# Transposing x and the adjacency on VectorE in 32x32 blocks instead of on TensorE

## The chip, the cores and the metric

One core of one Trainium2 chip. The metric is device time in microseconds (us) of one launch; lower is better. "Same" means within 2% of the other kernel.

## The reference, cut to what matters

128 graphs of 128 nodes and 768 features, one attention layer with 12 heads of 64 behind a layer norm and a relu, with the adjacency as bias and mask:

```python
h = jnp.maximum(_layernorm(x, axis=-1), 0.0)            # x: (128, 128, 768) float32
q, k, v = split(h @ Wq + bq), split(h @ Wk + bk), split(h @ Wv + bv)
scores = einsum('bhqd,bhkd->bhqk', q, k) / sqrt(64)
scores = where(adj > 0, scores + beta * adj, -9e15)      # adj: (128, 128, 128)
x = x + einsum('bhqk,bhkd->bhqd', softmax(scores), v)
```

## The kernel before

It works on groups of four graphs. The three projections run as "slices" (first half of q and k, then v, then second half of q and k); a slice is 15 block products of a fast matrix multiplication, each eight TensorE instructions into a PSUM bank. Each bank is emptied ("evicted") by VectorE or ScalarE before it is written again. The attention of the group and the preparation of the next group (layer norm, transposition of h, bias) are woven in between products. The parts:

```python
def norm(G, g):                                   # layer norm of one graph, rows on partitions
    for s in range(2):
        nc.vector.bn_stats(st[:, s, :], t[:, s * VH:(s + 1) * VH])
    nc.vector.bn_aggr(mv, st)
    nc.vector.tensor_scalar(ve, mv[:, 1:2], EPS, None, op0=ALU.add)
    nc.gpsimd.tensor_tensor(rstd, ve, nhalf, ALU.pow)            # 128x1
    nc.vector.tensor_scalar(t, t, mv[:, 0:1], rstd, op0=ALU.subtract, op1=ALU.mult)

def to_hT(G, r, k):                               # six a group
    for c in range(2):
        for g in range(2):
            nc.tensor.transpose(p[:, c, g, :], xg[G, 2 * r + g][:, at:at + P], ident)
    nc.scalar.activation(t, p..., AF.Relu)

# ... make_bias: cap and square the adjacency, then
    for g in range(GRP):
        nc.tensor.transpose(p[:, g, :], nb[:, g, :], ident)
    nc.scalar.activation(biasT[G], p, AF.Copy, scale=ISCALE)

def product(G, sl, n):                            # cut: eight matmuls into bank p, then for v
    # first use of an output block: out = bias +- p ; later uses: out = out +- p
    nc.vector.tensor_tensor(o, o, got, ALU.add if sign > 0 else ALU.subtract)
```

The code counts products from 0. The banks of a V slice are used in the order c, a, b, c, d, a, c, b, d, c, a, b, c, a, b. That is the order in which their evictions stand in VectorE's queue.

Of the kernel before, what the change touches and what calls it, by code (L numbers as in the profile page):

```python
# [9 lines left out]
F32 = mybir.dt.float32  # L10
I32 = mybir.dt.int32
U8 = mybir.dt.uint8
AF = mybir.ActivationFunctionType
# [82 lines left out]

@with_exitstack
def direct(ctx, tc, x, adj, wq, bq, wk, bk, wv, bv, beta, out, bad):

# [13 lines left out]
    ISCALE = math.sqrt(HD)  # L113
    assert N == P and 2 * HD == P and B % GRP == 0 and W == 512 and NC == 6 and GRP == 4
# [8 lines left out]
    def load_x(G, g):  # L123
        xg[G, g] = work.tile([P, D], F32, tag="x", name=f"x_{G}_{g}")
        nc.sync.dma_start(xg[G, g], x[G * GRP + g])
# [4 lines left out]
    make_identity(nc, ident)  # L130
    nhalf = const.tile([P, 1], F32, name="nhalf")
# [16 lines left out]
    def load_block(sl, k, j, t):  # L148
        rows = slice(k * 2 * P, (k + 1) * 2 * P)
        if sl == "v":  # L150
            nc.scalar.dma_start(t, wv[rows, j * 2 * P:(j + 1) * 2 * P].rearrange("(c p) n -> p c n", p=P))
        else:
            oc = j + 3 * int(sl[2])
            for i, w in enumerate((wq, wk)):
                nc.scalar.dma_start(t[:, :, i * P:(i + 1) * P],
                                    w[rows, oc * P:(oc + 1) * P].rearrange("(c p) n -> p c n", p=P))
# [23 lines left out]
    nc.scalar.dma_start(beta_c, beta[None, :].to_broadcast([P, 1]))  # L180
    bqk = const.tile([P, 2, NC], F32, name="bqk")
# [5 lines left out]

    def norm(G, g):
        t = xg[G, g]
        st = stat.tile([P, 2, nc.vector.BN_STATS_DIM], F32, tag="st", name=f"st_{G}_{g}")  # L190
        for s in range(2):
            nc.vector.bn_stats(st[:, s, :], t[:, s * VH:(s + 1) * VH])
        mv = stat.tile([P, nc.vector.BN_AGGR_DIM], F32, tag="mv", name=f"mv_{G}_{g}")
        nc.vector.bn_aggr(mv, st)
        ve = stat.tile([P, 1], F32, tag="ve", name=f"ve_{G}_{g}")
        nc.vector.tensor_scalar(ve, mv[:, 1:2], EPS, None, op0=ALU.add)
        rstd = stat.tile([P, 1], F32, tag="rstd", name=f"rstd_{G}_{g}")
        nc.gpsimd.tensor_tensor(rstd, ve, nhalf, ALU.pow)
        nc.vector.tensor_scalar(t, t, mv[:, 0:1], rstd, op0=ALU.subtract, op1=ALU.mult)

    def to_hT(G, r, k):
        p = psum.tile([P, 2, 2, N], F32, tag="at", name=f"pt_{G}_{r}_{k}")
        for c in range(2):
            for g in range(2):
                at = (2 * k + c) * P
                nc.tensor.transpose(p[:, c, g, :], xg[G, 2 * r + g][:, at:at + P], ident)  # L206
        t = work.tile([P, 2, H2], F32, tag="hT", name=f"hT_{G}_{r}_{k}", bufs=8)
        nc.scalar.activation(t, p.rearrange("p c g n -> p c (g n)"), AF.Relu)  # L208
        A[G, f"A{r}{k}"] = t
# [8 lines left out]
    def load_adj(G):  # L218
        a = work.tile([P, GRP, N], F32, tag="adj", name=f"adj_{G}", bufs=1)
        nc.sync.dma_start(a, adj[G * GRP:(G + 1) * GRP].rearrange("g q k -> q g k"))  # L220
        return a

    def make_bias(G, a):
        kp = work.tile([P, GRP, N], U8, tag="kp", name=f"kp_{G}", bufs=1)
        nc.vector.tensor_scalar(kp, a, 0.0, None, op0=ALU.is_gt)
        nc.vector.tensor_scalar(a, a, beta_c, BIAS_CAP, op0=ALU.mult, op1=ALU.min)
        nb = work.tile([P, GRP, N], F32, tag="nb", name=f"nb_{G}", bufs=1)
        nc.gpsimd.tensor_tensor(nb, a, a, ALU.mult)
        bm = stat.tile([P, GRP], F32, tag="bm", name=f"bm_{G}", bufs=1)
        nc.vector.tensor_reduce(bm, nb, AX.X, ALU.max)  # L230
        nc.vector.tensor_tensor(seen_b, seen_b, bm, ALU.max)
        nc.gpsimd.memset(nb, MASKED)
        nc.vector.copy_predicated(nb, kp, a)
        p = psum.tile([P, GRP, N], F32, tag="at", name=f"pb_{G}")
        for g in range(GRP):
            nc.tensor.transpose(p[:, g, :], nb[:, g, :], ident)  # L236

        biasT[G] = work.tile([P, GRP, N], F32, tag="biasT", name=f"biasT_{G}", bufs=2)
        nc.scalar.activation(biasT[G], p, AF.Copy, scale=ISCALE)  # L239
# [98 lines left out]
    for g in range(GRP):  # L338
        norm(0, g)
    for r, k in ((0, 1), (1, 0), (1, 1), (1, 2), (0, 0), (0, 2)):  # L340
        to_hT(0, r, k)
# [7 lines left out]
    for G in range(NG):  # L349
        todo = attention(G - 1, 1) if G else {}  # L350
        if not G:
            load_weights("v")
            for n in range(len(SUMS_B)):
                todo.setdefault(n, []).append(lambda n=n: sum_weights("v", n))
        slice_of(G, "qk0", todo)
        todo = {}
        if not G:
            load_weights("qk1")
            for n in range(len(SUMS_B)):
                todo.setdefault(n, []).append(lambda n=n: sum_weights("qk1", n))  # L360
        if G + 1 < NG:
            for g in range(GRP):
                load_x(G + 1, g)
                todo.setdefault(2 + 3 * g, []).append(lambda g=g: norm(G + 1, g))
            todo.setdefault(8, []).append(lambda: make_bias(G + 1, load_adj(G + 1)))
        slice_of(G, "v", todo)
        todo = attention(G, 0)
        if G + 1 < NG:
            for i, (r, k) in enumerate(((0, 1), (1, 0), (1, 1), (1, 2), (0, 0), (0, 2))):
# [150 lines left out]
```

## Time and profile before

| what | before |
|---|---|
| time, median of 4 | 3228.62 us (3228.18 to 3229.27) |
| a settled group | 99.01 us |
| first product of the run | at 27.50 us |
| third slice of the first group | at 92.96 us |
| TensorE / VectorE / ScalarE busy | 99% / 55% / 21% |

How to read it: a group's length is the distance between the first products of two successive qk1 slices. 32 groups make up the run, so 1 us a group is 1% of the time. Three groups of instructions, with columns line, engine, operation, output and input, shape, count, then total us and mean ns of one, then the idle time before them and what ended it:

```profile
L206 PE MATMUL pt<-ident,x 128*128 128x128 f32 x768 | 117.8, 278 | 18.4 <-DVE x L199 16.4 <-DVE ve L196 2.0
...
L199 DVE TENSOR_SCALAR x<-x,mv,rstd 128x768 f32<-128x768 f32 x128 | 91.0, 712 | 64.8 <-POOL rstd L198 64.7
...
L198 POOL TENSOR_TENSOR rstd<-ve,nhalf 128x1 f32<-128x1 f32 x128 | 70.9, 554 | 200.7 <-DVE ve L196 199.8 <-DMA x<-in_x_dram 0.9
```

GpSimd's power takes 0.554 us, and VectorE waits 64.7 us for it in the whole run, without TensorE waiting in the settled groups.

### The profile page before, as it was taken

The numbers are of one execution on the slowest core, as the hardware profiler recorded it, in microseconds if no ns is written. First come the engines' busy times: TensorE is split into PE (matmuls) and PEld (weight loads), VectorE is DVE, ScalarE is ACT, GpSimd is POOL, SyncE is SP. The second block draws the span as 40 slices with busy tenths as digits, with TensorE's granted clock in tenths as the row PEclk, the third lists the DMA queues.
The fourth block names the chain that finished last, engine by engine and source line by source line (L and its number), as shares of the span: only waits on it lengthen the run. The fifth ranks groups of instructions, "written<-read, shape, count | busy, mean of one in ns | idle before, by whom it ended". The sixth has DMA issues, their size and how long they took to land.

```text
span 3227.2 us, 46121 instructions
## 1 busy us (share of the span) xinstructions
PE 3185.1 (99%) x18562; PEld 2821.5 (87%) x18562; DVE 1777.4 (55%) x4516; ACT 677.1 (21%) x1377; POOL 546.4 (17%) x544
## 2 busy tenths in 40 slices
PE   6999999999999999999999999999999999999998
PEld 5888888888888888888888888888888888888887
DVE  8555455554555555555545555455555455554544
ACT  1221112212122121222121221212221112212121
POOL 4111121111111111111111111111111121111110
PEclk9999999999999999999999999999999999999998
DMA  5111121111121111211112111111111121111111
GB/s 152 56 50 53 33 62 57 50 52 38 55 60 50 55 50 36 59 56 50 56 30 63 60 50 53 45 44 59 56 50 53 33 63 56 51 52 35 51 40 31
DMA packets 252392, 169.88 MB, mean 53 GB/s; under 512 B 11152, under 2 KB 235664, under 8 KB 252176
## 3 DMA queue, kind: packets, MB, share of 16 engines
q1 hardware_dynamic: 238080, 159.42, 16.6%
q10 hardware_dynamic: 14096, 7.48, 0.9%
q8 instruction: 148, 2.42, 0.3%
q14 instruction: 68, 0.56, 0.1%
HBM read 116.53 MB, written 50.33 MB: 52 GB/s over the span
## 4 chain that ended last, share of the span: by engine, by line
PE 97%; DVE 1%; DMA 0%; POOL 0%; issue 0%; ACT 0%; ACTq 0%; POOLq 0%; DVEq 0%
PE pc_qk L257 17%; PE pb_qk L257 14%; PE pa_qk L257 14%; PE av L309 10%; PE pc_v L257 8%; PE pb_v L257 7%; PE pd_qk L257 7%; PE pa_v L257 7%; PE sc L296 7%; PE pd_v L257 3%; PE pt L206 3%; PE pb L236 0%; DMA qk_B<-in_L_gnn_Wk_dram 0%; DVE qk_T L176 0%; DVE v_T L176 0%
## 5 line engine op out<-in xcount | busy, mean ns | idle before, releaser
L320 POOL TENSOR_TENSOR xo<-xo,o 128x512 f32<-128x512 f32 x192 | 244.2, 1272 | 1722.5 <-DVE seen L318 1371.2
L309 PEld LDWEIGHTS av<-v,e 128*128 128x128 f32 x3072 | 377.6, 194 | 15.5 <-ACT e L300 5.3
L300 ACT ACTIVATE e<-e 128x512 f32<-128x512 f32 x384 | 235.7, 631 | 671.8 <-DVE e L299 671.8
L309 PE MATMUL av<-v,e 128*128 128x65 f32 x3072 | 369.3, 274 | 4.5 <-ACT e L300 4.5
L257 PE MATMUL pb_qk<-S,qk_T 128*128 128x256 f32 x1536 | 373.1, 386 | 0.0
L299 DVE SCALAR_TENSOR_TENSOR e<-sc,biasT 128x512 f32<-128x512 f32 x384 | 246.7, 684 | 162.2 <-PE sc L296 162.2
L278 ACT ACTIVATE qk<-pc_qk,bqk 128x256 f32<-128x256 f32 x384 | 161.0, 470 | 802.4 <-PE pc_qk L257 792.7
L282 DVE TENSOR_TENSOR qk<-qk,pb_qk 128x512 f32<-128x512 f32 x256 | 175.1, 684 | 264.5 <-PE pb_qk L257 245.9
L257 PEld LDWEIGHTS pb_qk<-S,qk_T 128*128 128x128 f32 x1536 | 279.3, 190 | 39.4 <-issue 0.3
L257 PE MATMUL pa_qk<-S,qk_T 128*128 128x256 f32 x1024 | 248.6, 386 | 0.0
L257 PE MATMUL pc_qk<-S,qk_B 128*128 128x256 f32 x1024 | 248.6, 386 | 0.0
L257 PE MATMUL pc_qk<-S,qk_T 128*128 128x256 f32 x1024 | 245.0, 383 | 2.9 <-DVE S L215 2.9
L296 PE MATMUL sc<-qk 64*128 64x128 f32 x3072 | 225.7, 286 | 0.0
L257 PEld LDWEIGHTS pc_qk<-S,qk_T 128*128 128x128 f32 x1024 | 194.0, 192 | 28.8 <-DVE S L215 3.3
L296 PEld LDWEIGHTS sc<-qk 64*128 64x128 f32 x3072 | 188.1, 188 | 30.2 <-issue 21.2
L257 PEld LDWEIGHTS pa_qk<-S,qk_T 128*128 128x128 f32 x1024 | 186.9, 190 | 29.2
L257 PEld LDWEIGHTS pc_qk<-S,qk_B 128*128 128x128 f32 x1024 | 186.9, 190 | 29.2
L239 ACT ACTIVATE biasT<-pb 128x512 f32<-128x512 f32 x32 | 19.1, 597 | 778.6 <-PE pb L236 778.6
L257 PE MATMUL pb_v<-v_T,S 128*128 128x256 f32 x768 | 181.4, 379 | 0.0
L257 PEld LDWEIGHTS pb_v<-v_T,S 128*128 128x128 f32 x768 | 145.9, 190 | 19.8
L315 DVE TENSOR_TENSOR o<-av,rs 128x256 f32<-128x256 f32 x384 | 161.8, 421 | 0.2
L215 DVE TENSOR_TENSOR S<-hT,hT 128x512 f32<-128x512 f32 x160 | 108.1, 692 | 97.6 <-ACT hT L208 97.6
(98 smaller groups left out, 4727.2 us busy)
## 6 DMA issues: line engine op xcount, KB each, us to landing
x<-in_x_dram SPq DMA_DIRECT2D x128, 384.0 KB, 4.3
xo<-in_x_dram SPq DMA_DIRECT2D x192, 256.0 KB, 2.8
out_dram<-xo SPq DMA_DIRECT2D x192, 256.0 KB, 2.3
adj<-in_adj_dram SPq DMA_DIRECT2D x32, 256.0 KB, 2.8
qk_B<-in_L_gnn_Wq_dram ACTq DMA_DIRECT2D x18, 128.0 KB, 3.5
qk_B<-in_L_gnn_Wk_dram ACTq DMA_DIRECT2D x18, 128.0 KB, 3.4
v_B<-in_L_gnn_Wv_dram ACTq DMA_DIRECT2D x9, 256.0 KB, 7.3
bv_b<-in_L_gnn_bv_dram ACTq DMA_DIRECT2D x1, 384.0 KB, 4.1
```

The lines of the kernel that those rows point to most:

```text
L206: nc.tensor.transpose(p[:, c, g, :], xg[G, 2 * r + g][:, at:at + P], ident)
L215: e.tensor_tensor(t, A[G, a], A[G, b], ALU.add if sign > 0 else ALU.subtract)
L239: nc.scalar.activation(biasT[G], p, AF.Copy, scale=ISCALE)
L257: nc.tensor.matmul(p[:, i, :], lhs, rhs, start=(first and i == 0 and c == 0), stop=(c == 1), skip_group_check=True)
L278: nc.scalar.activation(t[:, i, :], p[:, i, :], AF.Identity, bias=bqk[:, i, oc:oc + 1], scale=float(sign))
L282: nc.vector.tensor_tensor(t, t, p, ALU.add if sign > 0 else ALU.subtract)
L296: nc.tensor.matmul(ps[i][:, g, :], t[r, 1, at], t[r, 0, at], start=True, stop=True)
L299: nc.vector.scalar_tensor_tensor(e, ps[i], SCORE_CAP * ISCALE, biasT[G], op0=ALU.min, op1=ALU.add)
L300: nc.scalar.activation(e, e, AF.Exp, scale=1.0 / ISCALE)
L309: nc.tensor.matmul(pa[:, 2 * g + i, :], es[G, oc, i][:, 2 * r + g, :], vt[G, "v", r, h // 4][:, 4 * g + h % 4, :], start=True, stop=True)
L315: nc.vector.tensor_mul(o[:, r], pa[:, :, 0:HD], rs.to_broadcast([P, 4, HD]))
L320: nc.gpsimd.tensor_add(t, t, o.rearrange("p a (b j) d -> p (a b) (j d)", j=2))
```

## The change

Its intent: take 28 transposes a group (24 of x, 4 of the adjacency) off TensorE, the bound. x and the adjacency are loaded so that a partition holds pieces of rows in 32-row blocks, and VectorE transposes 32x32 blocks. A row's statistics are then spread over four partitions; two small matmuls with a constant matrix combine them. GpSimd's power turns the variance into the factor `rstd`, and `shift` is minus the mean times that factor. With both, ScalarE applies normalisation and relu in one instruction a block. The core of the diff:

```diff
+    def moments_1(G):                      # after product 5 of the V slice
+        nc.tensor.matmul(pm[G][:, 0], mean8..., halves(G, 1), start=True, stop=True)
+        ...
+    def moments_2(G, mean, d):             # after product 8
+        nc.tensor.matmul(pm[G][:, 1], mean8..., d, start=True, stop=True)
+        nc.vector.tensor_reduce(ve, pm[G][:, 1], AX.X, ALU.add)
+        nc.vector.tensor_scalar(ve, ve, EPS, None, op0=ALU.add)
+        nc.gpsimd.tensor_tensor(rstd[G], ve, nhalf.to_broadcast([P, GRP * NB]), ALU.pow)   # 128x16
+        nc.vector.scalar_tensor_tensor(shift[G], mean, -1.0, rstd[G], op0=ALU.mult, op1=ALU.mult)
     def norm(G, g):
-        ... bn_stats, bn_aggr, epsilon, power, tensor_scalar
+        for b in range(NB):
+            nc.scalar.activation(t, t, AF.Relu, bias=shift[G][:, n:n + 1], scale=rstd[G][:, n:n + 1])
     def to_hT(G, r, k):
-        ... four nc.tensor.transpose, one nc.scalar.activation
+        for g in range(2):
+            src = xg[G, 2 * r + g].rearrange("p b (j c) -> p c b j", c=NC)[:, 2 * k:2 * k + 2]
+            nc.vector.transpose(t[...], src)
     def make_bias(G, raw):
+        nc.vector.transpose(a, raw.rearrange("p g b j -> p g (b j)"))
-        ... four nc.tensor.transpose, one nc.scalar.activation
     # cut: loads of x and adj in four pieces each, weight rows permuted to match,
     # stats after products 0 to 3 of the V slice, x loads one slice earlier,
     # cut: transposes and sums of h at other products of the qk1 slice
```

The order of each engine's queue is settled when the program is built, from the order in the source and the data that each instruction needs; VectorE then executes its queue in that order.

More of the change, by code (lines that the diff above doesn't have):

```diff
@@ L94 @@
 SLICES = ("qk0", "v", "qk1")
+HT_AT = {"A01": 0, "A00": 1, "A11": 2, "A02": 3, "A10": 4, "A12": 9}
+HT_ORDER = tuple(HT_AT)
+SUMS_AT = (5, 9, 6, 6, 7, 8, 9, 10, 11, 13, 14)
 @with_exitstack
@@ L113, in direct @@
     ISCALE = math.sqrt(HD)
+    SQ = 32
+    NB = P // SQ
+    QD = D // NB
     assert N == P and 2 * HD == P and B % GRP == 0 and W == 512 and NC == 6 and GRP == 4
@@ L123, in load_x @@
     def load_x(G, g):
-        xg[G, g] = work.tile([P, D], F32, tag="x", name=f"x_{G}_{g}")
-        nc.sync.dma_start(xg[G, g], x[G * GRP + g])
+        t = xg[G, g] = work.tile([P, NB, QD], F32, tag="x", name=f"x_{G}_{g}")
+        src = x[G * GRP + g].rearrange("(b i) (a f) -> a i b f", i=SQ, a=NB)
+        for a in range(NB):
+            nc.sync.dma_start(t[a * SQ:(a + 1) * SQ], src[a])
     for g in range(GRP):
@@ L130, in direct @@
     make_identity(nc, ident)
+    fold = const.tile([P, SQ], F32, name="fold")
+    nc.vector.tensor_reduce(fold, ident.rearrange("p (a i) -> p i a", i=SQ), AX.X, ALU.add)
+    mean8 = const.tile([P, NB, SQ], F32, name="mean8")
+    nc.vector.tensor_scalar(mean8, fold[:, None, :].to_broadcast([P, NB, SQ]), 0.125, None, op0=ALU.mult)
     nhalf = const.tile([P, 1], F32, name="nhalf")
@@ L148, in load_block, with part @@
     def load_block(sl, k, j, t):
-        rows = slice(k * 2 * P, (k + 1) * 2 * P)
+        def part(w, at, n):
+            return w.rearrange("(p c) n -> p c n", c=NC)[:, 2 * k:2 * k + 2, at:at + n]
         if sl == "v":
-            nc.scalar.dma_start(t, wv[rows, j * 2 * P:(j + 1) * 2 * P].rearrange("(c p) n -> p c n", p=P))
+            nc.scalar.dma_start(t, part(wv, j * 2 * P, 2 * P))
         else:
@@ L154, in load_block @@
             for i, w in enumerate((wq, wk)):
-                nc.scalar.dma_start(t[:, :, i * P:(i + 1) * P],
-                                    w[rows, oc * P:(oc + 1) * P].rearrange("(c p) n -> p c n", p=P))
+                nc.scalar.dma_start(t[:, :, i * P:(i + 1) * P], part(w, oc * P, P))
     def load_weights(sl):
@@ L180, in direct @@
     nc.scalar.dma_start(beta_c, beta[None, :].to_broadcast([P, 1]))
+    nc.vector.tensor_scalar(beta_c, beta_c, ISCALE, None, op0=ALU.mult)
     bqk = const.tile([P, 2, NC], F32, name="bqk")
@@ L186, in direct @@
     nc.scalar.dma_start(bv_b, bv[None, :].to_broadcast([P, D]))
-    def norm(G, g):
-        t = xg[G, g]
-        st = stat.tile([P, 2, nc.vector.BN_STATS_DIM], F32, tag="st", name=f"st_{G}_{g}")
-        for s in range(2):
-            nc.vector.bn_stats(st[:, s, :], t[:, s * VH:(s + 1) * VH])
-        mv = stat.tile([P, nc.vector.BN_AGGR_DIM], F32, tag="mv", name=f"mv_{G}_{g}")
-        nc.vector.bn_aggr(mv, st)
-        ve = stat.tile([P, 1], F32, tag="ve", name=f"ve_{G}_{g}")
-        nc.vector.tensor_scalar(ve, mv[:, 1:2], EPS, None, op0=ALU.add)
-        rstd = stat.tile([P, 1], F32, tag="rstd", name=f"rstd_{G}_{g}")
-        nc.gpsimd.tensor_tensor(rstd, ve, nhalf, ALU.pow)
-        nc.vector.tensor_scalar(t, t, mv[:, 0:1], rstd, op0=ALU.subtract, op1=ALU.mult)
@@ L201, in to_hT @@
-    def to_hT(G, r, k):
-        p = psum.tile([P, 2, 2, N], F32, tag="at", name=f"pt_{G}_{r}_{k}")
-        for c in range(2):
-            for g in range(2):
-                at = (2 * k + c) * P
-                nc.tensor.transpose(p[:, c, g, :], xg[G, 2 * r + g][:, at:at + P], ident)
-        t = work.tile([P, 2, H2], F32, tag="hT", name=f"hT_{G}_{r}_{k}", bufs=8)
-        nc.scalar.activation(t, p.rearrange("p c g n -> p c (g n)"), AF.Relu)
-        A[G, f"A{r}{k}"] = t
+    st, pm, rstd, shift = {}, {}, {}, {}
@@ new lines, in stats, with halves @@
+    def stats(G, g):
+        if G not in st:
+            st[G] = stat.tile([P, GRP * NB, nc.vector.BN_STATS_DIM], F32, tag="st", name=f"st_{G}", bufs=2)
+        for b in range(NB):
+            nc.vector.bn_stats(st[G][:, g * NB + b, :], xg[G, g][:, b, :])
+    def halves(G, n):
+        return st[G].rearrange("p b (h m) -> p b h m", h=2)[:, :, :, n]
+    def moments_1(G):
+        pm[G] = psum.tile([P, 2, GRP * NB, 2], F32, tag="at", name=f"pm_{G}")
+        nc.tensor.matmul(pm[G][:, 0], mean8.rearrange("p a i -> p (a i)"), halves(G, 1), start=True, stop=True)
+        mean = stat.tile([P, GRP * NB], F32, tag="mean", name=f"mean_{G}", bufs=1)
+        nc.vector.tensor_reduce(mean, pm[G][:, 0], AX.X, ALU.add)
+        d = stat.tile([P, GRP * NB, 2], F32, tag="dev", name=f"dev_{G}", bufs=1)
+        nc.vector.tensor_tensor(d, halves(G, 1), mean[:, :, None].to_broadcast([P, GRP * NB, 2]), ALU.subtract)
+        nc.vector.tensor_tensor(d, d, d, ALU.mult)
+        nc.vector.scalar_tensor_tensor(d, halves(G, 2), 2.0 / QD, d, op0=ALU.mult, op1=ALU.add)
+        return mean, d
@@ new lines, in moments_2 @@
+    def moments_2(G, mean, d):
+        nc.tensor.matmul(pm[G][:, 1], mean8.rearrange("p a i -> p (a i)"), d, start=True, stop=True)
+        ve = stat.tile([P, GRP * NB], F32, tag="ve", name=f"ve_{G}", bufs=1)
+        nc.vector.tensor_reduce(ve, pm[G][:, 1], AX.X, ALU.add)
+        nc.vector.tensor_scalar(ve, ve, EPS, None, op0=ALU.add)
+        rstd[G] = stat.tile([P, GRP * NB], F32, tag="rstd", name=f"rstd_{G}", bufs=1)
+        nc.gpsimd.tensor_tensor(rstd[G], ve, nhalf.to_broadcast([P, GRP * NB]), ALU.pow)
+        shift[G] = stat.tile([P, GRP * NB], F32, tag="shift", name=f"shift_{G}", bufs=1)
+        nc.vector.scalar_tensor_tensor(shift[G], mean, -1.0, rstd[G], op0=ALU.mult, op1=ALU.mult)
@@ new lines, in norm @@
+    def norm(G, g):
+        for b in range(NB):
+            t = xg[G, g][:, b, :]
+            n = g * NB + b
+            nc.scalar.activation(t, t, AF.Relu, bias=shift[G][:, n:n + 1], scale=rstd[G][:, n:n + 1])
+    def to_hT(G, r, k):
+        name = f"A{r}{k}"
+        t = A[G, name] = work.tile([P, 2, H2], F32, tag=name, name=f"{name}_{G}", bufs=1 + (name in ("A01", "A02")))
+        for g in range(2):
+            src = xg[G, 2 * r + g].rearrange("p b (j c) -> p c b j", c=NC)[:, 2 * k:2 * k + 2]
+            nc.vector.transpose(t[:, :, g * N:(g + 1) * N].rearrange("p c (b i) -> p c b i", i=SQ), src)
@@ L218, in load_adj, with make_bias @@
     def load_adj(G):
-        a = work.tile([P, GRP, N], F32, tag="adj", name=f"adj_{G}", bufs=1)
-        nc.sync.dma_start(a, adj[G * GRP:(G + 1) * GRP].rearrange("g q k -> q g k"))
-        return a
-    def make_bias(G, a):
+        t = work.tile([P, GRP, NB, SQ], F32, tag="adj", name=f"adj_{G}", bufs=1)
+        src = adj[G * GRP:(G + 1) * GRP].rearrange("g (b i) (a j) -> a i (g b) j", i=SQ, a=NB)
+        for a in range(NB):
+            nc.sync.dma_start(t[a * SQ:(a + 1) * SQ].rearrange("p g b j -> p (g b) j"), src[a])
+        return t
+    def make_bias(G, raw):
+        a = work.tile([P, GRP, N], F32, tag="adjT", name=f"adjT_{G}", bufs=1)
+        nc.vector.transpose(a, raw.rearrange("p g b j -> p g (b j)"))
         kp = work.tile([P, GRP, N], U8, tag="kp", name=f"kp_{G}", bufs=1)
         nc.vector.tensor_scalar(kp, a, 0.0, None, op0=ALU.is_gt)
-        nc.vector.tensor_scalar(a, a, beta_c, BIAS_CAP, op0=ALU.mult, op1=ALU.min)
-        nb = work.tile([P, GRP, N], F32, tag="nb", name=f"nb_{G}", bufs=1)
-        nc.gpsimd.tensor_tensor(nb, a, a, ALU.mult)
+        nc.vector.tensor_scalar(a, a, beta_c, BIAS_CAP * ISCALE, op0=ALU.mult, op1=ALU.min)
+        t = biasT[G] = work.tile([P, GRP, N], F32, tag="biasT", name=f"biasT_{G}", bufs=2)
+        nc.gpsimd.tensor_tensor(t, a, a, ALU.mult)
         bm = stat.tile([P, GRP], F32, tag="bm", name=f"bm_{G}", bufs=1)
-        nc.vector.tensor_reduce(bm, nb, AX.X, ALU.max)
+        nc.vector.tensor_reduce(bm, t, AX.X, ALU.max)
         nc.vector.tensor_tensor(seen_b, seen_b, bm, ALU.max)
-        nc.gpsimd.memset(nb, MASKED)
-        nc.vector.copy_predicated(nb, kp, a)
-        p = psum.tile([P, GRP, N], F32, tag="at", name=f"pb_{G}")
-        for g in range(GRP):
-            nc.tensor.transpose(p[:, g, :], nb[:, g, :], ident)
-        biasT[G] = work.tile([P, GRP, N], F32, tag="biasT", name=f"biasT_{G}", bufs=2)
-        nc.scalar.activation(biasT[G], p, AF.Copy, scale=ISCALE)
+        nc.gpsimd.memset(t, MASKED)
+        nc.vector.copy_predicated(t, kp, a)
     banks = {}
@@ L338, in direct @@
     for g in range(GRP):
+        stats(0, g)
+    moments_2(0, *moments_1(0))
+    for g in range(GRP):
         norm(0, g)
-    for r, k in ((0, 1), (1, 0), (1, 1), (1, 2), (0, 0), (0, 2)):
-        to_hT(0, r, k)
+    for n in HT_ORDER:
+        to_hT(0, int(n[1]), int(n[2]))
     for n in range(len(SUMS_A)):
@@ L350, in direct, with then @@
         todo = attention(G - 1, 1) if G else {}
+        def then(n, f):
+            todo.setdefault(n, []).append(f)
         if not G:
@@ L353, in direct @@
             for n in range(len(SUMS_B)):
-                todo.setdefault(n, []).append(lambda n=n: sum_weights("v", n))
+                then(n, lambda n=n: sum_weights("v", n))
+        if G + 1 < NG:
+            for g in range(GRP):
+                then(11, lambda g=g: load_x(G + 1, g))
         slice_of(G, "qk0", todo)
@@ L359, in direct @@
             for n in range(len(SUMS_B)):
-                todo.setdefault(n, []).append(lambda n=n: sum_weights("qk1", n))
+                then(n, lambda n=n: sum_weights("qk1", n))
         if G + 1 < NG:
+            got = []
             for g in range(GRP):
-                load_x(G + 1, g)
-                todo.setdefault(2 + 3 * g, []).append(lambda g=g: norm(G + 1, g))
-            todo.setdefault(8, []).append(lambda: make_bias(G + 1, load_adj(G + 1)))
+                then(g, lambda g=g: stats(G + 1, g))
+                then(11 + g, lambda g=g: norm(G + 1, g))
+            then(5, lambda: got.extend(moments_1(G + 1)))
+            then(8, lambda: moments_2(G + 1, *got))
+            then(8, lambda: make_bias(G + 1, load_adj(G + 1)))
         slice_of(G, "v", todo)
@@ L368, in direct @@
         if G + 1 < NG:
-            for i, (r, k) in enumerate(((0, 1), (1, 0), (1, 1), (1, 2), (0, 0), (0, 2))):
-                todo.setdefault((2, 3, 4, 6, 7, 8)[i], []).append(lambda r=r, k=k: to_hT(G + 1, r, k))
-            for n in range(len(SUMS_A)):
-                todo.setdefault(max(8, n + 4), []).append(lambda n=n: sum_acts(G + 1, n))
+            for n, at in HT_AT.items():
+                then(at, lambda n=n: to_hT(G + 1, int(n[1]), int(n[2])))
+            for n, at in enumerate(SUMS_AT):
+                then(at, lambda n=n: sum_acts(G + 1, n))
         slice_of(G, "qk1", todo)
@@ L383, in direct @@
     nc.vector.tensor_scalar(over[:, 0:2], worst[:, 0:2], SUM_CAP, None, op0=ALU.is_gt)
-    nc.vector.tensor_scalar(over[:, 2:3], worst[:, 2:3], BIAS_CAP * BIAS_CAP, None, op0=ALU.is_ge)
+    nc.vector.tensor_scalar(over[:, 2:3], worst[:, 2:3], (BIAS_CAP * ISCALE) ** 2, None, op0=ALU.is_ge)
     pf = psum.tile([P, 4], F32, tag="mm", name="pf")
```

## The prediction

> **What bounds the kernel now.** I read the page first (busy shares, then the chain of work that ended last), then the TensorE timeline of one settled group of four graphs, then the start of the run, then the groups of instructions that the change touches.
>
> ```profile
> span 3227.2 us, 46121 instructions
> PE 3185.1 (99%) x18562; PEld 2821.5 (87%) x18562; DVE 1777.4 (55%) x4516; ACT 677.1 (21%) x1377; POOL 546.4 (17%) x544
> ...
> PE 97%; DVE 1%; DMA 0%; POOL 0%; issue 0%; ACT 0%; ACTq 0%; POOLq 0%; DVEq 0%
> PE pc_qk L257 17%; PE pb_qk L257 14%; PE pa_qk L257 14%; PE av L309 10%; PE pc_v L257 8%; PE pb_v L257 7%; PE pd_qk L257 7%; PE pa_v L257 7%; PE sc L296 7%; PE pd_v L257 3%; PE pt L206 3%; PE pb L236 0%; DMA qk_B<-in_L_gnn_Wk_dram 0%; DVE qk_T L176 0%; DVE v_T L176 0%
> ```
>
> TensorE is busy 99% of the span and carries 97% of the chain; everything else has slack, VectorE most of the load among it (55%). The transposes that the change takes away are "pt" (3%) and "pb" (under 0.5%). Busy time overlaps between pipelined matmuls, so what a transpose costs is read from starts, not durations:
>
> ```profile
> 1087.68 2.00 PE L257 MATMUL pb_qk<-S,qk_T 128*128 128x256 f32 x8
> 1089.52 0.60 PE L206 MATMUL pt<-ident,x 128*128 128x128 f32 x4
> 1089.95 1.89 PE L257 MATMUL pc_qk<-S,qk_T 128*128 128x256 f32 x8
> 1091.68 0.60 PE L206 MATMUL pt<-ident,x 128*128 128x128 f32 x4
> ...
> 1117.19 1.90 PE L309 MATMUL av<-v,e 128*128 128x65 f32 x16
> 1118.92 1.95 PE L257 MATMUL pb_qk<-S,qk_T 128*128 128x256 f32 x8
> 1120.70 1.89 PE L257 MATMUL pc_qk<-S,qk_T 128*128 128x256 f32 x8
> ...
> 1171.26 0.60 PE L236 MATMUL pb<-ident,nb 128*128 128x128 f32 x4
> 1171.69 1.89 PE L257 MATMUL pc_v<-v_B,S 128*128 128x256 f32 x8
> ```
>
> The reader sees no gap: each line starts where its neighbour lets it. From 1089.52 to 1091.68 is 2.16 us for four transposes and a product; a product alone repeats every 1.727 us in the V slice. So four transposes cost 0.44 us (x) or 0.43 us (adjacency, 1171.26 to 1171.69). A settled group takes 99.01 us, and these views show TensorE working through all of it:
>
> ```profile
> 1155.72:1182.06 26.34, 26.34 (x126) 23.19 (x125) 12.92 (x21) 0.60 (x1) 2.50 (x3) 1.00 0.10 30
> 1083.05:1182.06 99.01, 99.01 (x582) 87.81 (x581) 54.45 (x140) 21.12 (x43) 16.31 (x16) 1.00 0.18 51
> ```
>
> These are windows: length, then busy time of PE, PEld, DVE, ACT, POOL, then clock, DMA share, GB/s. The first is a V slice, the second a whole group. VectorE idles 13 us of the V slice and 44 us of the group.
>
> The start is another regime:
>
> ```profile
> 27.50 3.78 PE L257 MATMUL pc_qk<-S,qk_T 128*128 128x256 f32 x8 [2.94 <-DVE S L215]
> ...
> 43.02 1.09 PE L236 MATMUL pb<-ident,nb 128*128 128x128 f32 x4 [5.84 <-DVE nb L233]
> ...
> 92.96 1.89 PE L257 MATMUL pc_qk<-S,qk_T 128*128 128x256 f32 x8
> ```
> ```profile
> 8.00:12.00 4.00, 0.00 (x0) 0.00 (x0) 3.64 (x12) 0.00 (x0) 1.74 (x3) 1.00 1.14 317
> ```
>
> The first product starts at 27.5 us and the third slice of group 0 at 92.96. Thirty products would take 51.8 us, so group 0 loses some 13 us to waits and a cold clock. The DMA engines are full meanwhile (share 1.14, 317 GB/s).
>
> **What the Trainium skill says.** "TensorE: Matmul & The Clock Gate", section LDWEIGHTS (loading the stationary operand): a load takes its columns over 1.2 GHz, 107 ns for 128. The trace agrees: 16 "av" instructions and a product take 3.51 us (1117.19 to 1120.70), less 1.727 this is 0.111 us an instruction although only 65 columns stream. "Vector Engine (DVE) Microarchitecture Reference", section 3.8: the 32x32 transpose sustains one element per cycle per lane. No run here shows it yet. "ScalarE: Activation LUTs", section What ACT_TABLE_LOAD costs: 186 ns, 93 ns for each per-partition pointer, 0.833 ns an element, neighbours overlapping by 93 ns. The trace has 470 ns for 128x256 with one pointer where that gives 492, and pairs in 0.84 us, so it is near. "DMA: Bandwidth & Descriptors", section Why small descriptors are slow: a fixed overhead for each packet. Nearly all packets of the kernel before are 512 B and more, so the trace can't say what the 128 B runs of the new adjacency load cost.
>
> **The change part by part.** Removed from TensorE, counted after 92.96 us: 31 sets of 24 x transposes, 31 x 6 x 0.44 = 81.8 us, and 30 sets of adjacency transposes, 30 x 0.43 = 12.9 us; together 94.7 us, all of it on the chain. Added to TensorE: two fp32 matmuls a group (128x128 stationary, 32 columns), two instructions each as every fp32 matmul here, bound by the weight load: 4 x 0.111 = 0.45 us, 30 times 13.4 us. Net 81.3 us saved.
>
> VectorE, per group. Removed: normalising, 4 x 0.71 = 2.8 us; bn_stats 8 x 0.53 = 4.2; the aggregation and epsilon 4 x 0.34 = 1.4. Added: 12 transposes of 256 elements; a 512-element tensor_tensor takes 0.684 us of which 0.533 are elements at 0.96 GHz, so I take 0.267 + 0.15 = 0.42 us, 5.0 us; one adjacency transpose 0.69; bn_stats 16 x 0.33 = 5.3 (half the elements of 0.53); some eight tiny operations, 1.3. Net about +3.9 us on 54.5, to 58 of 96. ScalarE, per group. Removed: 7 evictions of 0.60 = 4.2 us. Added: 16 relus of 192 elements with two pointers, 0.44 us apart by the skill's figures: 7.0 us. Both stay far from full.
>
> The built order moves more than the diff tells. Ten of the twelve transposes stand in the last third of the V slice, between evictions, and the x load of the next group starts as soon as they let a tile go. I walked VectorE's queue from the second moments matmul on: shift is ready about 1.8 us after the ninth V product, the relus of tile n at 3.8, 5.5, 7.1, 8.8 us, and each eviction between the transposes ends at most 1.8 us after its product. A PSUM bank is written again after two other products, 3.45 us, so TensorE doesn't wait. The adjacency load is issued a whole group ahead of its use; the 49.6 us that VectorE waited for it disappear but cost nothing before.
>
> At the start the order turns bad. VectorE's in-order queue now holds all V weight sums and the first qk1 weight sum ahead of the row statistics' end. So the first normalisation waits for x (1.57 MB), the qk0 and V weights (2.36 each), the V bias (0.39), four qk1 pieces (0.52) and half an adjacency (0.13): 7.3 MB. At 300 GB/s that is 24 us, some 28 with the first latency and eight DMAs in flight at a time. About 3.5 us more go to the second moment, pow and shift. Then VectorE works through 12 transposes (5.0), the bias (3.4) and three sums (2.1) before the first product can start: 28 + 3.5 + 11 = 42.5, with GpSimd in its way (VectorE sums stretch from 0.68 to 1.75 us beside GpSimd in this start) about 45. Against 27.5 that is 17 us late. In return the V sums are done, and group 0 should flow: 51.8 plus 0.5 for the moments, 1.7 for the cold clock and 3 for backlog give 57 instead of 65.5. So the third slice starts at 102 instead of 93: 9 us given back.
>
> Sum: 3227.2 - 81.3 + 9 = 3155 us of span; the timed run is 1.8 us longer (3228.96 against 3227.2): 3157 us, 2.2% faster.
>
> **The rivals.** (1) VectorE becomes a wait in the settled groups. For it: transposes, statistics and evictions share one in-order queue; if a transpose takes two cycles an element (0.69 us), evictions end up to 2.6 us late. Against it: the 3.45 us of bank reuse, 44 us idle a group. It would cost 0.5 to 1 us a group, time 3175 to 3190. (2) DMA: x comes in 768 B runs and the adjacency in 128 B runs, 2048 packets each a group instead of 512; a late tile blocks VectorE's queue at bn_stats. Against it: DMA share 0.18, and bn_stats of a tile stands some 4 us after the issue. If tiles land in 8 us instead, 2 to 3 us of blocking, partly hidden: up to 3190. (3) The start is much better or worse: with the sums waiting less, or group 0 flowing fully, 3148; with small packets halving the DMA rate, 15 us more, 3172. (4) The moments matmuls cost more than their weight loads, because a short stream can't hide the next load: 0.3 us a group more, 3166.
>
> **Range and chances.** The saving of 94.7 us is read directly and sure. The best case, no loss at the start and no wait, is 3148. Terms that can go wrong mostly add: 5 us at the start, 5 in the moments, 10 in small waits. So 3147 to 3175 for 8 in 10. The 2% line is 3164.4, only 7 us above my number, so faster 0.68, same 0.29, slower 0.03.
>
> **What would show it.** A settled group of about 96.4 us instead of 99.01, with products still 1.727 us apart and no gap longer than 0.1 us in the V slice; "pm" steps of 0.22 us; transposes of 0.42 us on VectorE; first product near 45 us and the third slice near 102 us. I am wrong if groups differ by less than 2 us (a new wait), if waits of TensorE on VectorE appear in every group, or if the start is late by more than 15 us at 92.96.

## The result, and the profile after

3211.53 us, median of 4 runs (3210.15 to 3213.84), against 3228.62 us. Ratios here are the mean time of one kernel's fast runs over that of the other's of the same rounds, so not quite the ratio of the medians; this one is 0.9948, 95% interval 0.993 to 0.9965. It is 0.5% faster where 2.2% was forecast, and the time lies outside the forecast range. From the page of the kernel after, busy time and the chain by engine:

```profile
PE 3109.2 (97%) x17794; PEld 2737.0 (85%) x17794; DVE 1962.6 (61%) x5031; ACT 781.5 (24%) x1665; POOL 571.2 (18%) x448
...
PE 87%; DVE 5%; POOL 3%; issue 1%; DMA 1%; ACT 1%; ACTq 0%; POOLq 0%; DVEq 0%
```

TensorE's share of the chain fell from 97% to 87%: something else now holds the run up. GpSimd, which had no part in it, holds 3%. The TensorE timeline of the end of a settled V slice shows where (start, length, then in brackets the idle time before and what ended it):

```profile
1180.78 1.89 PE L305 MATMUL pb_v<-v_T,A 128*128 128x256 f32 x8
1182.51 1.89 PE L305 MATMUL pc_v<-v_T,A 128*128 128x256 f32 x8
1185.28 1.99 PE L305 MATMUL pa_v<-v_B,S 128*128 128x256 f32 x8 [0.88 <-DVE v L321]
1187.44 1.99 PE L305 MATMUL pb_v<-v_T,S 128*128 128x256 f32 x8 [0.17 <-DVE v L321]
1189.27 1.89 PE L305 MATMUL pc_qk<-S,qk_T 128*128 128x256 f32 x8
```

A product should follow every 1.727 us. From pc_v to pa_v it is 2.77, from pa_v to pb_v 2.16, from pb_v to the next slice 1.83: 1.58 us too much. The previous group's qk1 slice began at 1091.31, so a group takes 97.96 us; 97.96 - 1.58 is 96.38, the forecast's group. The two products wait for evictions by VectorE. Its timeline in the same stretch:

```profile
1178.13 0.18 DVE L241 TENSOR_SCALAR ve<-ve 128x16 f32<-128x16 f32 x1
1181.39 0.17 DVE L245 SCALAR_TENSOR_TENSOR shift<-mean,rstd 128x16 f32<-128x16 f32 x1 [3.08 <-POOL rstd L243]
1181.48 0.68 DVE L321 TENSOR_TENSOR v<-v,pc_v 128x512 f32<-128x512 f32 x1
1183.49 1.16 DVE L258 STREAM_TRANSPOSE A<-x 128x256 f32<-128x256 f32 x2 [1.33 <-ACT x L251]
1184.57 0.65 DVE L321 TENSOR_TENSOR v<-v,pa_v 128x512 f32<-128x512 f32 x1
1185.13 1.68 DVE L258 STREAM_TRANSPOSE A<-x 128x256 f32<-128x256 f32 x3
1186.72 0.67 DVE L321 TENSOR_TENSOR v<-v,pb_v 128x512 f32<-128x512 f32 x1
```

VectorE stands still for 3.08 us at the shift, because GpSimd's power is not done. The eviction of pc behind it could have run some 2.2 us earlier (elsewhere an eviction starts 0.2 us after the next product does, and that product started at 1179.06). Then VectorE waits another 1.33 us for ScalarE's first relus, which also wait for the shift. The eviction of pa ends at 1185.22 and pa_v starts at 1185.28; pb's ends at 1187.39 and pb_v starts at 1187.44. So the chain is power, shift, relus, transposes, evictions, products. The groups of instructions behind it:

```profile
L258 DVE STREAM_TRANSPOSE A<-x 128x256 f32<-128x256 f32 x384 | 222.0, 618 | 77.7 <-ACT x L251 41.3 <-PE pa_qk L305 36.4
...
L243 POOL TENSOR_TENSOR rstd<-ve,nhalf 128x16 f32<-128x16 f32 x32 | 93.0, 2905 | 501.4 <-DVE ve L241 501.4
```

Sixteen powers a partition take 2.905 us where one took 0.554, and a transpose takes 0.618 us where 0.42 was forecast. At the start, TensorE's timeline reads:

```profile
31.90 0.64 PE L227 MATMUL pm<-st,mean 128*128 128x32 f32 x2 [31.90 <-DVE st L219]
36.00 0.64 PE L238 MATMUL pm<-dev,mean 128*128 128x32 f32 x2 [3.46 <-DVE dev L233]
...
52.71 3.78 PE L305 MATMUL pc_qk<-S,qk_T 128*128 128x256 f32 x8 [16.08 <-DVE S L264]
```

The first product comes at 52.71 instead of 27.50 us, and the third slice at 111.67 instead of 92.96. The run's span of 3208.3 us is thus accounted for against the forecast's 3155: the third slice 9.7 us later than the forecast's 102, 30 later V slices with 1.58 us of waits each, 47.4 us, and 3.6 us less from the last slice's start to the end (61.8 against 65.4 us), where after the last product some small matmuls of the kernel before ran slower (12 score instructions in 1.65 us from 3203.63, in the kernel after 0.94 from 3186.78). The granted clock read 0.50 over those of the kernel before and 1.00 over those of the kernel after. It falls to 0.50 in both ends, only sooner in the kernel before; the other runs' ends take 61.3 to 65.1 us, so these 3.6 us look like luck: no run shows the change at work in them. 9.7 + 47.4 - 3.6 = 53.5, and the difference is 53.3.

### The profile page after: what moved, and what is told of

Its sections match the earlier page's. It is cut to its first block, busy times and chain, and to the rows that moved or that the text cites. A ratio compares the mean times of both kernels' runs of the same rounds, so it can differ in the third digit from the quotient of the medians.

```text
span 3208.3 us, 46341 instructions
## 1 busy us (share of the span) xinstructions
PE 3109.2 (97%) x17794; PEld 2737.0 (85%) x17794; DVE 1962.6 (61%) x5031; ACT 781.5 (24%) x1665; POOL 571.2 (18%) x448
## 4 chain that ended last, share of the span: by engine, by line
PE 87%; DVE 5%; POOL 3%; issue 1%; DMA 1%; ACT 1%; ACTq 0%; POOLq 0%; DVEq 0%
PE pc_qk L305 18%; PE pb_qk L305 14%; PE pa_qk L305 14%; PE av L357 10%; PE pd_qk L305 7%; PE sc L344 7%; PE pb_v L305 5%; PE pc_v L305 5%; PE pa_v L305 3%; PE pd_v L305 3%; POOL rstd L243 3%; DVE A L258 2%; DVE v L321 2%; ACT x L251 1%; DMA v_B<-in_L_gnn_Wv_dram 0%
## 5 line engine op out<-in xcount | busy, mean ns | idle before, releaser
L251 ACT ACTIVATE x<-x,shift,rstd 128x192 f32<-128x192 f32 x512 | 227.8, 533 | 902.8 <-DVE shift L245 902.8
L258 DVE STREAM_TRANSPOSE A<-x 128x256 f32<-128x256 f32 x384 | 222.0, 618 | 77.7 <-ACT x L251 41.3
L330 DVE TENSOR_TENSOR qk<-qk,pd_qk 128x512 f32<-128x512 f32 x128 | 88.0, 687 | 181.2 <-PE pd_qk L305 181.2
L264 POOL TENSOR_TENSOR S<-S,A 128x512 f32<-128x512 f32 x64 | 81.8, 1278 | 642.4 <-PE pa_qk L305 614.2
```

The lines of the kernel that those rows point to most:

```text
L251: nc.scalar.activation(t, t, AF.Relu, bias=shift[G][:, n:n + 1], scale=rstd[G][:, n:n + 1])
L258: nc.vector.transpose(t[:, :, g * N:(g + 1) * N].rearrange("p c (b i) -> p c b i", i=SQ), src)
L264: e.tensor_tensor(t, A[G, a], A[G, b], ALU.add if sign > 0 else ALU.subtract)
L330: nc.vector.tensor_tensor(t, t, p, ALU.add if sign > 0 else ALU.subtract)
```

## The experiments

The theory: the power of 2.9 us, not the 0.55 that the kernel before suggested, makes the shift late and blocks VectorE's queue. "Rival 2" in the expectations is the forecast's own first rival: transposes of 0.62 us are too much for VectorE by themselves. "Theory 3" concerns the start.

**Is it the power's duration?** Two edits, one that takes the cost away (the result is wrong: relative error 0.26) and one that doubles it.

```diff
-        nc.gpsimd.tensor_tensor(rstd[G], ve, nhalf.to_broadcast([P, GRP * NB]), ALU.pow)
+        nc.gpsimd.tensor_tensor(rstd[G], ve, nhalf.to_broadcast([P, GRP * NB]), ALU.mult)
```

> A wrong result on purpose: GpSimd multiplies where it took the power, on the same 128x16 elements with the same operands; nothing else moves. Theory 1: the multiplication takes under 0.5 us instead of 2.9, the shift comes about 2.4 us earlier, TensorE's waits at the end of the V slice go, a settled group is 96.3 to 96.9 us, and the time is 3160 to 3180 us. Rival 2 (slow transposes): waits of TensorE stay at 0.7 us or more a group and the time stays above 3195 us.

Measured: 3161.50 us, ratio to the kernel before 0.9797 (0.978 to 0.9813). From this run's groups of instructions, the multiplication:

```profile
L243 POOL TENSOR_TENSOR rstd<-ve,nhalf 128x16 f32<-128x16 f32 x32 | 6.9, 216 | 501.4 <-DVE ve L241 501.4
```

0.216 instead of 2.905 us; a settled group is 96.38 us (1072.04 to 1168.42) and no wait of TensorE on v is left in the settled groups. The doubling:

```diff
+        nc.gpsimd.tensor_tensor(twice, ve, nhalf.to_broadcast([P, GRP * NB]), ALU.pow)
         nc.gpsimd.tensor_tensor(rstd[G], ve, nhalf.to_broadcast([P, GRP * NB]), ALU.pow)
```

> The kernel after with the suspected cost doubled: GpSimd takes the power of 128x16 twice, once into a spare tile; VectorE's order is the same. Theory 1: the shift waits 6.0 instead of 3.08 us, nothing of the added 2.9 us is hidden any more, so TensorE's waits grow by 2.6 to 2.9 us a group, a settled group is 100.6 to 100.9 us, and the time is 3290 to 3302 us with the 2.9 us at the start. If GpSimd's power is not on the path that sets the group, the time stays within 15 us of 3211.

Measured: 3298.45 us, ratio 1.0218 (1.0201 to 1.0235), groups that alternate between 100.32 and 101.05 us, 2.7 us more than 97.96 on average; the shift waits 5.88 us. The order was not quite the same as I had written: one eviction of pb stood one transpose earlier in VectorE's queue. The power lies on the path that sets the group, and nearly all of what is added to it is paid.

**Does it help to run it earlier?** The statistics after product 0, the moments after products 2 and 5, nothing else.

```diff
-                then(g, lambda g=g: stats(G + 1, g))
+                then(0, lambda g=g: stats(G + 1, g))
-            then(5, lambda: got.extend(moments_1(G + 1)))
-            then(8, lambda: moments_2(G + 1, *got))
+            then(2, lambda: got.extend(moments_1(G + 1)))
+            then(5, lambda: moments_2(G + 1, *got))
```

> The same work, but the row statistics stand after the first V product, the first moments matmul after the third and the second after the sixth, so that the power and the shift come three products (5 us) earlier in the queues. Theory 1 (the 2.9 us power of GpSimd holds up VectorE's in-order queue, and the late evictions make TensorE wait 1.05 us in each V slice, with about 0.5 us more of smaller losses): the waits of pa_v and pb_v on VectorE fall to under 0.2 us a group, a settled group takes 96.3 to 96.9 us instead of 97.96, and the time is 3165 to 3180 us. Rival 2 (the transposes at 0.62 instead of 0.42 us are what delays the evictions): the same twelve transposes stand between the same evictions, so the waits stay at 0.7 us or more a group and the time stays above 3195 us. The start is not touched: first product near 52.7 us either way.

Measured: 3208.33 us, ratio 0.994 (0.9923 to 0.9956): a miss of my theory as I had put it. The group is 97.87 us. TensorE's one wait, and VectorE's:

```profile
1182.69 1.99 PE L305 MATMUL pc_v<-v_T,A 128*128 128x256 f32 x8 [1.22 <-DVE v L321]
```
```profile
1171.75 0.17 DVE L241 TENSOR_SCALAR ve<-ve 128x16 f32<-128x16 f32 x1
1175.01 0.18 DVE L245 SCALAR_TENSOR_TENSOR shift<-mean,rstd 128x16 f32<-128x16 f32 x1 [3.08 <-POOL rstd L243]
```

VectorE's wait is as long as before, 3.08 us, and TensorE's only moved to the product before. "Late" was the wrong word: the shift stands directly behind the power's input in VectorE's queue, so VectorE has nothing to do meanwhile, whenever that is. The Trainium skill, "DVE: scalar operands, raw-bit mode, write accounting and state across instructions", section 5, Flops that outlive an instruction, says that VectorE's queue "is one in-order queue"; the 3.08 us with an eviction ready behind the shift agree. The sharper theory: the place of the shift is what costs.

**The place of the shift.** First on top of the early moments, the shift behind the eviction of the eighth product:

```diff
+            def late_shift():
+                with tc.issue_after(ev[G, 7].ins):        # queue order only, no wait
+                    make_shift(G + 1, got[0])
+            then(7, late_shift)
```

> The early moments once more (the statistics after product 0, moments after products 2 and 5 of the V slice), and the shift is now queued on VectorE behind the eviction of the eighth product, two evictions after the power was started, instead of directly behind its input. The run before it showed that without this the 3.08 us wait only moves: pc_v waits 1.22 us in place of pa_v's 0.88 and pb_v's 0.17. Theory 1 as it now stands (what costs is not when the power runs but that VectorE's next instruction in the queue is the shift, so that two evictions stand still behind it): the shift's wait falls from 3.08 to under 0.7 us, TensorE's waits on v go, a settled group is 96.3 to 96.7 us, and the time is 3155 to 3170 us. Rival 2 (twelve transposes of 0.62 us between the evictions are too much for VectorE whatever the power does): a wait of 0.4 us or more a group stays, and the time is over 3178 us. The start is as before, first product 52 to 53.5 us.

Measured: 3163.28 us, ratio 0.9797 (0.9781 to 0.9813), a correct result. No settled group has a wait of TensorE on v any more, and a group is 96.38 us. Then the decisive one, with the moments where the change has them and the shift alone moved, behind the eviction of the eleventh product; the transposes, which need it, follow:

```diff
-        nc.vector.scalar_tensor_tensor(shift[G], ...)        # in moments_2, behind the power
+            def late_shift():
+                with tc.issue_after(ev[G, 10].ins):
+                    make_shift(G + 1, got[0])
+            then(10, late_shift)
```

> The kernel after with its moments where they were (after products 0 to 3, 5 and 8) and only the shift moved: it is queued on VectorE behind the eviction of the eleventh product, two evictions after the power was started, instead of directly behind its input. Theory 1 (what costs is the shift's place in VectorE's in-order queue, not how early the power runs): the shift waits under 0.6 us, the evictions of pc and pa run on time while GpSimd takes the power, TensorE's waits on v fall below 0.2 us a group, a settled group is 96.3 to 96.7 us and the time is 3158 to 3172 us, as with the early moments. If the power must also run earlier, because the relus and transposes now end after the V slice, waits of TensorE appear in the first products of the qk1 slice and the time stays above 3180 us.

Measured: 3163.30 us, ratio 0.98 (0.9784 to 0.9816). VectorE's timeline and the window of one group (length, then busy time of PE, PEld, DVE, ACT, POOL):

```profile
1160.88 0.18 DVE L241 TENSOR_SCALAR ve<-ve 128x16 f32<-128x16 f32 x1
1162.00 0.69 DVE L323 TENSOR_TENSOR v<-v,pc_v 128x512 f32<-128x512 f32 x1 [0.95 <-PE pc_v L307]
1163.73 0.69 DVE L323 TENSOR_TENSOR v<-v,pa_v 128x512 f32<-128x512 f32 x1 [1.04 <-PE pa_v L307]
1164.34 0.17 DVE L247 SCALAR_TENSOR_TENSOR shift<-mean,rstd 128x16 f32<-128x16 f32 x1
1165.46 0.69 DVE L323 TENSOR_TENSOR v<-v,pb_v 128x512 f32<-128x512 f32 x1 [0.95 <-PE pb_v L307]
1166.43 1.70 DVE L260 STREAM_TRANSPOSE A<-x 128x256 f32<-128x256 f32 x3 [0.29 <-ACT x L253]
```
```profile
1074.05:1170.44 96.39, 96.39 (x558) 85.53 (x557) 60.42 (x157) 24.39 (x53) 17.08 (x13) 1.00 0.19 53
```

The power runs as long as ever, from 1161.20 on in GpSimd's timeline, but now two evictions run beside it, and the shift does not wait at all. The transposes of 0.6 us are as many and as long, and even end after the V slice; TensorE is busy through all 96.39 us. So rival 2 falls as a sufficient cause, and the place of one instruction of 0.17 us was worth 1.5% of the run. The transposes moved down the queue with the shift, so this run alone does not separate the two; mult_for_pow does: there eight transposes stand between the same evictions as in the kernel after, and its group is 96.38 us as well.

**Do the long transposes take part?** They read every sixth element. With neighbouring elements (wrong, relative error 0.21):

```diff
-            src = xg[G, 2 * r + g].rearrange("p b (j c) -> p c b j", c=NC)[:, 2 * k:2 * k + 2]
+            src = xg[G, 2 * r + g].rearrange("p b (c j) -> p c b j", c=NC)[:, 2 * k:2 * k + 2]
```

> A wrong result on purpose: the transposes read neighbouring elements instead of every sixth one; shapes and order are the same. Theory 1: each transpose falls from 0.62 to about 0.42 us (256 elements[...] plus 0.15), but the shift is as late as before, so 0.7 to 1.0 us of TensorE's wait per group stays and the time is 3190 to 3210 us. Rival 2: with the transposes at the 0.42 us of the forecast the waits go and the time is 3160 to 3180 us. If the transposes stay at 0.62 us, the stride is not what makes them slow.

Measured: 3185.31 us, ratio 0.9869 (0.9852 to 0.9885), between the two expectations and in neither. The transposes, and the product that still waits:

```profile
L258 DVE STREAM_TRANSPOSE A<-x 128x256 f32<-128x256 f32 x384 | 153.9, 427 | 90.1 <-ACT x L251 64.0 <-PE pa_qk L305 22.5
```
```profile
1174.45 1.99 PE L305 MATMUL pa_v<-v_B,S 128*128 128x256 f32 x8 [0.49 <-DVE v L321]
```

The stride makes them slow: 427 instead of 618 ns. A group is 97.17 us (1080.87 to 1178.04), so about half of the 1.58 us goes with it. Once VectorE is behind, its work decides how fast it catches up; the two causes overlap, and removing the standstill alone removes all.

**Does cutting the power help?** Four powers of 128x4, each followed by its own shift:

```diff
+        for g in range(GRP):
+            c = slice(g * NB, (g + 1) * NB)
+            nc.gpsimd.tensor_tensor(rstd[G][:, c], ve[:, c], nhalf.to_broadcast([P, NB]), ALU.pow)
+            nc.vector.scalar_tensor_tensor(shift[G][:, c], mean[:, c], -1.0, rstd[G][:, c], ...)
```

> One power of 128x16 is cut into four of 128x4, each with its own shift. Theory 1 with a cost by element (0.55 us for one element, 2.9 for sixteen: 0.4 fixed and 0.16 an element): each takes about 1.0 us, but VectorE's queue holds the four shifts in a row and the relus of the first graph start some 1.9 us earlier, while the last shift is about 1.2 us later, so the queue of VectorE is held at least as long: 3205 to 3225 us. If the cost is by instruction and not by element (each 2.9 us), the four take 11 us and the time rises over 3330 us. Rival 2 expects no change beyond 10 us.

Measured: 3201.60 us, ratio 0.9918 (0.9901 to 0.9934), 3 us below the expected range. Each power takes 1.010 us, so with 0.554 for one element and 2.905 for 16 the cost is about 0.40 us and 0.157 us an element. VectorE stands still longer in sum, four waits of 1.19, 0.82, 0.81 and 0.81 us, but the first relus start earlier and the 1.33 us wait before the transposes is gone, which I had not counted. A group is 97.59 us.

**The parts alone.** The kernel before with the adjacency part:

```diff
+        for a in range(NB):                                   # load_adj: four pieces, 32-row blocks
+            nc.sync.dma_start(t[a * SQ:(a + 1) * SQ]..., src[a])
+        nc.vector.transpose(a, raw...)                        # make_bias
-        nc.tensor.transpose(p[:, g, :], nb[:, g, :], ident)   # four
-        nc.scalar.activation(biasT[G], p, AF.Copy, scale=ISCALE)
```

> The kernel before with the adjacency part of the change alone (32-row blocks, one VectorE transpose of 512 elements, no TensorE transpose, no ScalarE eviction); x as before. The forecast's sum gives 30 times 0.43 = 12.9 us, and no new wait: a settled group 98.58 instead of 99.01 us, the time 3212 to 3219 us. If the 128-byte runs of the load or the extra VectorE work cost anything that TensorE sees, the group stays above 98.8 us and the time above 3222 us.

Measured: 3210.80 us, ratio 0.9947 (0.9931 to 0.9964): better than expected, and as much as the whole change. The group is 98.57 us, as forecast; the rest is a third slice at 88.91 instead of 92.96 us, and an end that is 2.0 us shorter. And the x part, the same diff in reverse on the kernel after:

> The x part of the change alone: the kernel after with the adjacency as before (512-byte rows, four TensorE transposes and a ScalarE eviction a group). The adjacency part alone gained 17.9 us (3228.7 to 3210.8) and the whole change 17.1 us. If the parts add up, the x part alone gains next to nothing: a settled group 98.3 to 98.5 us (97.96 plus 0.43), pa_v and pb_v wait for v as in the kernel after, the first product is as late as there (50 us or later), and the time is 3222 to 3232 us. If the adjacency's VectorE work is what fills the queue, the waits of TensorE on v fall below 0.5 us a group and the time is under 3218 us. At the start, without the 128-byte runs, the DMA rate between 4 and 12 us tells whether the 768-byte runs of x by themselves lower it: the kernel before and the adjacency alone show 308 to 351 GB/s there, the kernel after 252.

Measured: 3234.20 us, ratio 1.0019 (1.0002 to 1.0036), 2 us above the expected range; the group is 98.69 us, where 97.96 + 0.43 is 98.39. The x part, which takes 24 of the 28 transposes off TensorE, lost slightly more than it gained. The parts do not quite add: 17.9 gained and 5.5 lost make 12.4, and the whole gained 17.1. In the x part alone TensorE's wait of 0.88 us comes one product earlier than in the kernel after, and the step behind it takes 2.07 instead of 1.727 us; why was not tried.

**The start.** The weights of V and of the third slice on the queue of x, behind x and the adjacency:

```diff
-            nc.scalar.dma_start(t, part(wv, j * 2 * P, 2 * P))
+            nc.sync.dma_start(t, part(wv, j * 2 * P, 2 * P))
-                nc.scalar.dma_start(t[...], part(w, oc * P, P))
+                (nc.scalar if sl == "qk0" else nc.sync).dma_start(t[...], part(w, oc * P, P))
```

> Only the start is touched: the weights of V and qk1 come on the queue of x, behind x and the adjacency, so VectorE's queue holds the statistics and transposes ahead of the V sums. Theory 3 (the start is late because the statistics stand behind V weight sums that wait for 7 MB of loads): x (1.57 MB), an adjacency and the qk0 weights (2.36 MB) land by 20 us, the power starts by 26 us, the first product by 38 to 42 us instead of 52.7, and the third slice starts 12 to 17 us earlier than 111.7; the time is 3195 to 3201 us. Rival (the loads are slow because x now comes in 768-byte packets): the statistics of x_3 stay at 29 us or later and the first product at 50 us or later; the time stays at 3210 us. The settled group stays at 97.96 us in either case.

Measured: 3197.68 us, ratio 0.9907 (0.989 to 0.9923). TensorE's timeline:

```profile
22.31 0.64 PE L227 MATMUL pm<-st,mean 128*128 128x32 f32 x2 [22.31 <-DVE st L219]
23.91 0.64 PE L238 MATMUL pm<-dev,mean 128*128 128x32 f32 x2 [0.97 <-DVE dev L233]
40.76 3.63 PE L305 MATMUL pc_qk<-S,qk_T 128*128 128x256 f32 x8 [16.21 <-DVE S L264]
```

Statistics 9.6 us earlier, first product 12 us earlier, third slice at 98.28 instead of 111.67. The loads were not faster: from 8 to 12 us the DMA engines moved 248 GB/s here and 253 in the kernel after. So the order, not the rate, cost these 13 us. But the edit changed two orders at once. In the kernel after, the last load of x was issued at 23.9 us, in between those of V's weights, and took 5.2 us to land; here it was issued at 18.1 and took 2.9. That is 8.1 of the 9.6 us; at most the other 1.5 come from the V sums that stood ahead of the last statistics in VectorE's queue. The two were not tried apart. The rate did fall with the change (317 GB/s before); the x part alone shows 261 there and the adjacency part 308, so in that window it is the loads of x that lower it. What that costs of the remaining 5.3 us (98.28 against 92.96) was not tried.

**Both together**, the early moments with the moved shift, and the weights moved (the diffs of late_shift and vqk1_on_sync together):

> The same as the run before in this call, and the V and qk1 weights are loaded on the x queue behind x and the adjacency. If the two losses (the power's wait in each settled group, the V weight sums ahead of the statistics at the start) are separate and add up, it gains on the run before what vqk1_on_sync gains on the changed kernel: 12 to 17 us, to 3140 to 3155 us, 2.3 to 2.7% faster than the kernel before. If both fight for VectorE in group 0 it gains less than 8 us.

Measured: 3150.02 us (3148.66 to 3150.79), ratio 0.9758 (0.9742 to 0.9775), a correct result. It is 13.3 us below the moved shift alone, where the weights alone gave 13.9: the two losses are separate and add up. This version beats both kernels in every run.

## Why the prediction was wrong

- **TensorE's saving: right.** Without waits a group is 96.38 to 96.39 us in four runs; the forecast's terms give 99.01 - 3.07 + 0.45 = 96.39. A moments matmul costs 0.22 us, as forecast: the two steps between products around it are 1.86 and 1.81 us instead of 1.727.
- **The walk of VectorE's queue: the step that failed.** "Shift is ready about 1.8 us after the ninth V product" was mis-sized: that product ended near 1177.3 and the shift ran at 1181.39, 4.1 us later. The 1.8 us has room for a power as short as in the kernel before, 0.55 us on 128x1; on 128x16 it took 2.905. I carried a duration to sixteen times the elements and did not ask what stood behind the waiting instruction. "Each eviction between the transposes ends at most 1.8 us after its product" fell with it: pa's ended 4.3 us after its product (1180.95 to 1185.22). "So TensorE doesn't wait" became 1.58 us in each of 31 V slices. Moving the shift (late_only) gave 48 us back. (The forecast also has ten of the twelve transposes in the V slice; the trace has eight there.)
- **VectorE's transposes: too small a term.** 0.618 us instead of 0.42 for x, by the stride of six; the contiguous adjacency transpose took 0.704 against 0.69 forecast. Worth half of the wait, but only while the standstill is there.
- **Rival 1: its sign right, its cause half right.** "VectorE becomes a wait in the settled groups" at 0.5 to 1 us a group is what came, at 1.58, with the power as the main cause, which it did not name.
- **The start: mechanism right in part, sizes off.** The statistics did stand behind the V sums, but x's own last load, at 29.1 us, was most of the delay. The wait forecast at 28 us was 31.9; "3.5 us to the second moment, pow and shift" was 8.4, of which the power is 2.9; the work to the first product took 12.4 instead of 13.5 us. With 59.0 instead of 57 us for the 30 products that is 9.7 us more. (What the forecast calls the cold clock is a granted clock that reads 0.50 from 40 to 44 us in the kernel before; the product at 43.90 took 3.07 us there.)
- **ScalarE and the settled loads: right.** 16 relus took 7.12 us, 0.44 apart as forecast, and VectorE waited for x only 1.9 us in the whole run.
- **The chances.** I gave "small waits" 10 us of room because VectorE idled 44 us a group. Idle time of an in-order engine is no reserve where it stands still at a wait with urgent work behind it.

## What to carry to other kernels

When a change widens an instruction on another engine, measure that instruction at its new width before trusting a schedule, and look at what stands in the consumer's in-order queue directly behind the wait. If the producer is slow, put independent work between issuing it and using its result; here one 0.17 us instruction, two evictions later with the work that needs it, was worth 48 us, while running the producer earlier was worth 3. At a start, order the loads so that what the first product needs is not queued behind loads and sums for a later slice.

## What the Trainium skill lacked or had wrong

- "GPSIMD Engine Reference", section 3.1, Elementwise — side-by-side cycle accounting, gives about 2.6 cycles an element for a two-input add and nothing for a power. The runs: a multiplication of 128x16 took 0.216 us, the power 0.554, 1.010 and 2.905 us for 1, 4 and 16 elements a partition, so about 0.157 us an element.
- "Vector Engine (DVE) Microarchitecture Reference", section 3.8, says that the 32x32 transpose sustains one element per cycle per lane. With neighbouring source elements the trace agrees (0.427 us for 256 elements, 0.704 for 512, so 1.08 ns an element); with every sixth element read it was 0.618 us for 256, and the section says nothing of strides. Section 5.2 of the same page, Measured stream behaviour on trn2, does have slower rates for streams that step every element, of another operation; it has none for a transpose.
- "DMA: Bandwidth & Descriptors", section Why small descriptors are slow, counts a fixed overhead of about 3 cycles a packet, beside one cycle for each 32 bytes; for runs of 768 bytes that is an estimate of 11%, and 3% for the 3072-byte rows of x before. The load rate from 8 to 12 us fell from 317 to 261 GB/s with the x part alone, 18%. What makes the difference is open, as the loads' order changed too.
